# A four-layer gated decoder on one core: layer 2's expert features spread over the partitions, every eleventh into a chunk

## The chip, the core and the metric

The kernel runs as one program on one core of a Trainium2 chip. The metric is the device time of an execution in microseconds (us); the median of 13 runs of the kernel before is 1903.45 us, from 1896.32 to 1908.32. Beside these runs one execution was profiled, and every line of a profile below comes from it.

The names of the engines in the profile: PE is TensorE's matmul, PEld its weight load, DVE is VectorE, ACT is ScalarE, POOL is GpSimd, SP is SyncE, which issues most of the transfers. L1906 is line 1906 of the kernel.

## What is computed

64 sequences of 64 tokens with 128 features go through four layers. Each layer adds a gated attention branch to `x` and then a gated feed-forward branch, every branch on a layernorm of `x`. The change touches layer 2's feed-forward branch: a router picks two of eight experts for a token, every expert is a gated unit of 176 hidden features, and a ninth, shared expert is weighted by a sigmoid.

```python
def _L2_ffn_ref(hidden_states, gate_w, w_gate, w_up, w_down, sw_gate, sw_up, sw_down, shared_gate_w):
    E, K, I = (8, 2, 176)
    ...
    combine = jnp.sum(jax.nn.one_hot(topk_i, E, dtype=topk_w.dtype) * topk_w[..., None], axis=1)
    g = jnp.einsum('th,ehi->eti', x, w_gate)
    u = jnp.einsum('th,ehi->eti', x, w_up)
    eo = jnp.einsum('eti,eih->eth', jax.nn.silu(g) * u, w_down)
    out = jnp.einsum('te,eth->th', combine, eo)
    sg = jax.nn.sigmoid(jnp.einsum('th,oh->to', x, shared_gate_w))
    so = jax.nn.silu(x @ sw_gate) * (x @ sw_up) @ sw_down
    out = out + sg * so
```

The kernel computes all nine experts for every token. The nine times 176 features are one row of 1584 features, and each feature's hidden value is multiplied by its expert's weight for the token (zero for an expert that was not picked) ahead of the down projection.

## The kernel before, in words

**Groups, units and the planner.** The 4096 tokens are eight groups of 512 (4 tiles of 128). There are eight steps: 0, 2, 4 and 6 are the attention branches of layers 0 to 3, and 1, 3, 5 and 7 the feed-forward ones. A unit is one step of one group. The list `ORDER` (L2135) names the units in the order in which they are recorded: "50" is step 5, layer 2's feed-forward branch, of group 0. Nothing runs while units are recorded. Every operation goes into a plan (L299), which knows from the tiles what each operation depends on. `Plan.order` (L401) then writes one instruction stream for each engine: it walks through time with an estimated duration for each operation (`cost`, L221), and gives each engine the operation of the lowest rank that is ready, where the rank is essentially the place in the recording. So operations of several groups and layers stand mixed on each engine, and the engines run them in exactly the order that was written. Scratch tiles come from pools of fixed size (`SLOTS`, L41): 45 tiles of 2 KB a partition (in the profile `b2k`), 8 banks of PSUM (`ps`), and others; an operation that opens a tile waits in the plan until one is free. Where the plan sees TensorE idle, `keep_clock` (L482) fills the gap with matmuls of the identity into a free bank, which nobody reads; they carry line L2158.

**Layer 2's feed-forward unit** (L1896). `ln_T` normalizes and transposes the group into `xT`, 128 features by 512 tokens. `route` (L1847) computes the nine weights of each token, mostly on DVE. `spread` (L1885) transposes them (L1889), copies them out of PSUM (ACT, L1891) and writes them to a DRAM scratch `cwd` of 9 rows by 512 tokens (SP, L1893). Then come 13 chunks of features. In the kernel before, chunk c holds the features 128c to 128c+127 (the last one 48). A chunk's tile `cb` of 128 by 512 has in partition r the weight row of feature r's expert; it is loaded from `cwd` with one broadcast for each expert in the chunk (L1906), two or one a chunk, 20 a unit. A chunk is then two matmuls (L1914 and L1915, gate and up; one, L1911, for the last chunk), Silu on ACT (L1917), the product with the up part on DVE (L1918), the product with `cb` on POOL (L1919), and the down projection on TensorE (L1920), which accumulates over the chunks in one bank. The sum is copied out (L1922), transposed and added to `x`.

**The weights** (L1816) are loaded once. `wg` and `wu` lie as 128 input features by 1584 columns, and a chunk's stationary operand is 128 neighbouring columns of it. `wd` lies as 13 blocks of 128 features; L1833 loads it with 29 transfers.

Other lines that are spoken of below: L1236 and L1291 are layer 0's expert matmuls, and L1282 issues the loads of its one-hot rows (DRAM scratch `ohd`), which the products of L1289 read. L840 is the transpose of any step. L1663, L1674 and L1701 are the attention matmuls of layers 2 and 3. L1585 issues layer 1's feed-forward gathers from POOL, eight a unit.

Of the kernel before, what the change touches and what calls it, by code (L numbers as in the profile page):

```python
# [27 lines left out]
P = 128  # L28
# [5 lines left out]
GT = 512  # L34
# [730 lines left out]
def bc(ap, axis, n):  # L765

    ap = ap.unsqueeze(axis)
    shape = list(ap.shape)
    shape[axis] = n
    return ap.to_broadcast(shape)  # L770
# [8 lines left out]
def first_onehot(k, vals, best, rank, tag):  # L779

    nc = k.nc
    p, m, n = vals.shape
    eq = k.tile([p, m, n], tag=tag + "e")
    nc.vector.tensor_tensor(eq, vals, bc(best, 2, n), ALU.is_equal)
    nc.vector.tensor_tensor(eq, eq, bc(rank, 1, m), ALU.mult)
    top = k.tile([p, m], tag=tag + "t")
    nc.vector.tensor_reduce(top, eq, AX.X, ALU.max)
    oh = k.tile([p, m, n], tag=tag + "o")  # L790
    nc.vector.tensor_tensor(oh, eq, bc(top, 2, n), ALU.is_equal)
    return oh
# [42 lines left out]
def transpose4(k, src):  # L835

    ps = k.ps()
    k.plan.wait(src)
    for t in range(4):
        k.nc.tensor.transpose(ps[:, t * P : (t + 1) * P], src[:, t, :], k.ident)  # L840
    return ps


def ln_T(k, g):

    ps = transpose4(k, layernorm(k, g))
    xT = k.tile([P, GT], tag="xT")
    k.nc.scalar.copy(xT, ps)
    return xT
# [966 lines left out]
def l2_ffn_weights(k):  # L1816
    k.l2f = {"gate": k.load("l2f_gate")}

    last = k.l2f["last"] = k.fixed("w_l2f_last", [P, 112])
    k.nc.gpsimd.memset(last, 0.0)  # L1820
    at, end = k.done
    for n, name in enumerate(("wg", "wu")):
        t = k.l2f[name] = k.fixed("w_l2f_" + name, [P, 1536])
        k.nc.scalar.dma_start(out=t, in_=k.a["l2f_" + name][:, :1536])
        k.nc.scalar.dma_start(out=last[:, 64 * n : 64 * n + 48], in_=k.a["l2f_" + name][:, 1536:])
        k.plan.after = k.plan.ops[at + (end - at) * (n + 1) // 3]
    src = k.a["l2f_wd"]
    wd = k.l2f["wd"] = k.fixed("w_l2f_wd", [P, 13, P])
    for n in range(18):
        r = 88 * n  # L1830
        while r < 88 * n + 88:
            end = min(88 * n + 88, (r // P + 1) * P)
            k.nc.sync.dma_start(  # L1833
                out=wd[r % P : r % P + end - r, r // P, :], in_=src[r - 88 * n : end - 88 * n, n * P : (n + 1) * P]
            )
            r = end


def l2_ffn(k):
    nc = k.nc  # L1840
    E, I, HID = 8, 176, 9 * 176
    CH = [(c, min(P, HID - c)) for c in range(0, HID, P)]
    W = k.l2f

    gate = k.tg[:, 1, 2:3]

    def route(xT, g):  # L1847

        pr = k.ps()
        for t in range(TG):  # L1850
            nc.tensor.matmul(
                pr[:, t * (E + 1) : (t + 1) * (E + 1)], xT[:, t * P : (t + 1) * P], W["gate"], start=True, stop=True
            )
        lg = pr[:, : TG * (E + 1)].rearrange("p (t e) -> p t e", e=E + 1)
        pb = k.tile([P, TG, E], tag="pb")
        m = k.tile([P, 4, TG], tag="m")
        nc.vector.tensor_reduce(m[:, 0], lg[:, :, 0:E], AX.X, ALU.max)
        nc.vector.tensor_tensor(pb, lg[:, :, 0:E], bc(m[:, 0], 2, E), ALU.subtract)
        nc.scalar.activation(pb, pb, AF.Exp)
        nc.vector.tensor_reduce(m[:, 1], pb, AX.X, ALU.add)  # L1860
        nc.vector.reciprocal(m[:, 1], m[:, 1])
        nc.vector.tensor_tensor(pb, pb, bc(m[:, 1], 2, E), ALU.mult)
        nc.vector.tensor_reduce(m[:, 2], pb, AX.X, ALU.max)
        oh1 = first_onehot(k, pb, m[:, 2], k.rank8, tag="l2oh1")
        nc.vector.scalar_tensor_tensor(pb, oh1, -2.0, pb, ALU.mult, ALU.add)
        nc.vector.tensor_reduce(m[:, 3], pb, AX.X, ALU.max)
        oh2 = first_onehot(k, pb, m[:, 3], k.rank8, tag="l2oh2")

        nc.vector.tensor_tensor(m[:, 0], m[:, 2], m[:, 3], ALU.add)
        nc.vector.reciprocal(m[:, 0], m[:, 0])  # L1870
        nc.vector.scalar_tensor_tensor(m[:, 2], m[:, 2], gate, m[:, 0], ALU.mult, ALU.mult)
        nc.vector.scalar_tensor_tensor(m[:, 3], m[:, 3], gate, m[:, 0], ALU.mult, ALU.mult)
        cw = k.tile([P, TG, E + 1], tag="cw")
        nc.vector.tensor_tensor(oh1, oh1, bc(m[:, 2], 2, E), ALU.mult)
        nc.vector.tensor_tensor(oh2, oh2, bc(m[:, 3], 2, E), ALU.mult)
        nc.vector.tensor_tensor(cw[:, :, 0:E], oh1, oh2, ALU.add)

        sg = k.tile([P, TG], tag="sg1")
        nc.scalar.activation(sg, lg[:, :, E], AF.Exp, scale=-1.0)
        nc.vector.tensor_scalar(sg, sg, 1.0, None, ALU.add)  # L1880
        nc.vector.reciprocal(sg, sg)
        nc.vector.tensor_scalar(cw[:, :, E], sg, gate, None, ALU.mult)
        return cw

    def spread(cw):  # L1885

        pc = k.ps()
        for t in range(TG):
            nc.tensor.transpose(pc[: E + 1, t * P : (t + 1) * P], cw[:, t, :], k.ident)  # L1889
        cT = k.tile([E + 1, GT], tag="cwT")  # L1890
        nc.scalar.copy(cT, pc[: E + 1, :])  # L1891
        d = k.dram([E + 1, GT], "cwd")
        nc.sync.dma_start(out=d, in_=cT)  # L1893
        return d

    def unit(g):  # L1896
        xT = ln_T(k, g)
        cwd = spread(route(xT, g))
        py = k.ps()
        for c, (c0, cn) in enumerate(CH):  # L1900
            cb = k.tile([P, GT], tag="cb")
            r = c0
            while r < c0 + cn:
                e = r // I
                end = min(c0 + cn, (e + 1) * I)
                nc.sync.dma_start(out=cb[r - c0 : end - c0, :], in_=cwd[e : e + 1, :].to_broadcast([end - r, GT]))  # L1906
                r = end
            pg = k.ps()
            if cn < P:
                pu = pg[64 : 64 + cn]  # L1910
                nc.tensor.matmul(pg[: 64 + cn], W["last"], xT, start=True, stop=True)  # L1911
            else:
                pu = k.ps()
                nc.tensor.matmul(pg, W["wg"][:, c0 : c0 + cn], xT, start=True, stop=True)  # L1914
                nc.tensor.matmul(pu, W["wu"][:, c0 : c0 + cn], xT, start=True, stop=True)  # L1915
            h = k.tile([P, GT], tag="h")
            nc.scalar.activation(h[:cn], pg[:cn], AF.Silu)  # L1917
            nc.vector.tensor_tensor(h[:cn], h[:cn], pu, ALU.mult)  # L1918
            nc.gpsimd.tensor_tensor(h[:cn], h[:cn], cb[:cn], ALU.mult)  # L1919
            nc.tensor.matmul(py, W["wd"][:cn, c, :], h[:cn], start=(c == 0), stop=(c == len(CH) - 1))  # L1920
        yT = k.tile([P, TG, P], tag="yT")
        nc.scalar.copy(yT.rearrange("p t i -> p (t i)"), py)  # L1922
        xg = k.x[g].rearrange("p t d -> p (t d)")
        nc.vector.tensor_tensor(xg, xg, transpose4(k, yT), ALU.add)

    return unit
# [44 lines left out]
def l3_ffn(k):  # L1971
# [163 lines left out]
ORDER = [  # L2135
    (int(n), int(g))
    for n, g in (
        "02 00 03 01 06 04 10 05 11 20 07 21 30 31 40 12 41 50 13 51 16 22 14 60 15 61 23 70 26 32 17 24 "
        "71 42 25 33 36 27 43 34 46 52 35 44 62 45 37 53 56 47 63 54 66 55 64 65 72 57 67 73 76 74 75 77"
    ).split()  # L2140
]

# [1 line left out]
def program(tc, a):  # L2144
    with ExitStack() as es:
# [9 lines left out]
        for g in early:  # L2155
            nc.sync.dma_start(out=k.x[g], in_=xin[g])
        constants(k)
        plan.spare = (sys._getframe().f_lineno, k.ident, k.ident.t.writes[-1][0])  # L2158
        mixers = (l0_xattn, l0_ffn, l1_xattn, l1_ffn, l2_xattn, l2_ffn, l3_xattn)
        weights = (None, l0_ffn_weights, l1_xattn_weights, l1_ffn_weights, l2_xattn_weights, l2_ffn_weights,  # L2160
                   l3_xattn_weights)
        layers = [None] * 8
# [123 lines left out]
```

## Time and profile before

| | |
|---|---|
| median of 13 runs | 1903.45 us (1896.32 to 1908.32) |
| the profiled execution's own time | 1901.54 us |
| its span in the profile | 1899.8 us |
| mean granted TensorE clock | 0.975 of full speed |
| busy: PE, DVE, ACT, POOL | 1809.8, 1361.8, 1106.2, 1023.9 us |
| moved by DMA | 121.11 MB |

The span is what the profile's views add up to; the execution's own time is 1.7 us longer, and the median of the runs another 1.9 us. A line of the groups names the source line, the engine and operation, the tiles, the shapes and the count, then the busy time and the mean duration of one in ns, and last the idle time of the engine just ahead of it with what ended it. One float32 matmul in the program appears as two weight loads and two passes. [...]

### The profile page before, as it was taken

How to read it: one execution, taken by the hardware profiler on the slowest of the kernel's cores; microseconds unless marked ns; L12 is line 12 of the kernel's file. 1: busy time of each engine (PE TensorE's matmuls, PEld its weight loads, DVE VectorE, ACT ScalarE, POOL GpSimd, SP SyncE). 2: the span in 40 equal slices, each digit the busy share in tenths (PEclk: the TensorE clock that was granted, in tenths of full speed). 3: DMA queues.
4: the chain of work that ended last, by engine and by line, in shares of the span. 5: the costliest groups of instructions: out<-in, count | busy, mean ns of one | idle time of the engine just before them, and what ended most of it. 6: DMA issues, size and time to landing. Idle time of an engine off the chain costs nothing.

```text
span 1899.8 us, 44771 instructions
## 1 busy us (share of the span) xinstructions
PE 1809.8 (95%) x16701; PEld 1067.0 (56%) x16703; DVE 1361.8 (72%) x3194; ACT 1106.2 (58%) x2957; POOL 1023.9 (54%) x1655
## 2 busy tenths in 40 slices
PE   7999999999999999999999999999799999999996
PEld 4555456655555454655566655584466555555675
DVE  6786887678767477557786668769558876855567
ACT  6564446745374253733458743877467766867655
POOL 7772446644352443412638354856577478466546
PEclk8899999998999999999999999999899999999999
DMA  6302231013333321031210022000140034153121
GB/s 189 115 22 82 57 95 26 2 36 108 104 75 109 102 54 65 9 91 48 73 49 13 10 55 79 24 3 1 40 118 29 29 98 120 34 137 100 33 74 45
DMA packets 122231, 121.11 MB, mean 64 GB/s; under 512 B 58378, under 2 KB 78485, under 8 KB 122013
## 3 DMA queue, kind: packets, MB, share of 16 engines
q1 hardware_dynamic: 112541, 102.66, 19.2%
q10 hardware_dynamic: 6400, 9.25, 1.6%
q0 software_dynamic: 3072, 6.33, 1.2%
q8 instruction: 132, 2.16, 0.5%
q14 instruction: 86, 0.70, 0.1%
HBM read 98.22 MB, written 8.18 MB: 56 GB/s over the span
## 4 chain that ended last, share of the span: by engine, by line
PE 69%; DVE 9%; POOL 8%; ACT 4%; DMA 4%; issue 3%; another core or an unknown queue 1%; SPq 0%; ACTq 0%; DVEq 0%; POOLq 0%
PE ps L1236 11%; PE ps L1291 8%; PE ps L840 8%; POOL b L776 6%; PE ps L1920 5%; PE ps L1914 4%; PE ps L1915 4%; PE ps L1470 3%; PE ps L1701 3%; PE ps L1349 3%; PE ps L1457 2%; PE ps L1663 2%; PE ps L1386 2%; PE ps L1263 1%; DVE b2k L1289 1%
## 5 line engine op out<-in xcount | busy, mean ns | idle before, releaser
L776 POOL TENSOR_TENSOR b<-b,neghalf 128x8 f32<-128x8 f32 (+1 forms) x208 | 303.2, 1458 | 17.0
L1291 PE MATMUL ps<-b2k,w_l0f_oe 128*128 128x512 f32 x512 | 234.2, 601 | 3.6 <-DVE b2k L1289 2.4
L1236 PE MATMUL ps<-w_l0f_ve,b2k 128*128 128x512 f32 x512 | 236.3, 602 | 0.5 <-DVE b4k L1105 0.2
L775 POOL TENSOR_SCALAR b<-b 128x8 f32<-128x8 f32 (+1 forms) x208 | 44.3, 213 | 317.9 <-DVE b L804 193.2
L1289 DVE TENSOR_TENSOR b2k<-b2k,b2k 128x512 f32<-128x512 f32 x256 | 173.9, 729 | 28.1 <-PE ps L1291 13.3
L1242 DVE COPY_PREDICATED b2k<-b1k,ps 128x512 f32<-128x512 int32 x224 | 162.0, 727 | 43.4 <-PE ps L1236 25.7
L1919 POOL TENSOR_TENSOR b2k<-b2k,b2k 128x512 f32<-128x512 f32 (+1 forms) x104 | 130.8, 1281 | 106.7 <-DMA b2k<-cwd 59.0
L1104 DVE TENSOR_REDUCE b<-ps 128x8 f32<-128x512 f32 x224 | 146.9, 683 | 56.0 <-PE ps L1674 14.8
L1291 PEld LDWEIGHTS ps<-b2k,w_l0f_oe 128*128 128x128 f32 x512 | 93.7, 191 | 121.1 <-issue 80.6
L1107 ACT ACTIVATE b4k<-b4k 128x64 f32<-128x64 f32 x512 | 125.8, 250 | 47.1 <-DVE b4k L1105 44.4
L1105 DVE TENSOR_TENSOR b4k<-ps,b 128x512 f32<-128x512 f32 x224 | 149.5, 683 | 3.1 <-PE ps L840 2.2
L1236 PEld LDWEIGHTS ps<-w_l0f_ve,b2k 128*128 128x128 f32 x512 | 93.5, 191 | 101.8 <-issue 84.1
L840 PE MATMUL ps<-ident,b2k 128*128 128x128 f32 x896 | 133.6, 277 | 9.7 <-DVE b2k L1360 3.4
L840 PEld LDWEIGHTS ps<-ident,b2k 128*128 128x128 f32 x896 | 102.5, 141 | 68.9 <-issue 33.0
L840 PE MATMUL ps<-ident,b4k 128*128 128x128 f32 x896 | 127.8, 279 | 6.9 <-DVE b2k L1918 1.9
L840 PEld LDWEIGHTS ps<-ident,b4k 128*128 128x128 f32 x896 | 102.7, 142 | 51.2 <-issue 28.6
L1918 DVE TENSOR_TENSOR b2k<-b2k,ps 128x512 f32<-128x512 f32 (+1 forms) x104 | 70.2, 684 | 73.1 <-ACT b2k L1917 38.6
L1360 DVE TENSOR_TENSOR b2k<-ps,b 128x512 f32<-128x512 f32 x128 | 87.5, 687 | 30.7 <-POOL b L1357 17.0
L1354 DVE TENSOR_REDUCE b<-b2k 128x8 f32<-128x512 f32 x128 | 84.9, 678 | 27.8 <-ACT b2k L1351 25.0
L1920 PE MATMUL ps<-b2k,w_l2f_wd 128*128 128x512 f32 (+1 forms) x208 | 102.0, 608 | 2.9 <-POOL b2k L1919 2.8
L1689 ACT ACTIVATE b4k<-b4k 128x512 f32<-128x512 f32 x128 | 76.2, 630 | 48.2 <-DVE b4k L1105 47.8
L1440 POOL TENSOR_TENSOR b4k<-b4k,b 128x512 f32<-128x512 f32 x64 | 67.6, 1078 | 65.5 <-DVE b L1437 54.4
(368 smaller groups left out, 4090.0 us busy)
## 6 DMA issues: line engine op xcount, KB each, us to landing
b2k<-ohd SPq DMA_DIRECT2D x256, 128.0 KB
b2k<-cwd SPq DMA_DIRECT2D x40, 256.0 KB
b2k<-in_ctxT SPq DMA_DIRECT2D x32, 256.0 KB
b2k<-b2k SPq DMA_DIRECT2D x128, 64.0 KB
b2k<-b2k SPq DMA_DIRECT2D x32, 128.0 KB
b2k<-cwd SPq DMA_DIRECT2D x16, 224.0 KB
b2k<-cwd SPq DMA_DIRECT2D x16, 192.0 KB
b2k<-cwd SPq DMA_DIRECT2D x16, 160.0 KB
```

What stands on the lines that cost most here:

```text
L776: k.nc.gpsimd.tensor_tensor(out, out, k.neghalf[:, :n], ALU.pow)
L840: k.nc.tensor.transpose(ps[:, t * P : (t + 1) * P], src[:, t, :], k.ident)
L1104: nc.vector.tensor_reduce(mx, src, AX.X, ALU.max)
L1105: nc.vector.tensor_tensor(out, src, bc(mx, 2, S), ALU.subtract)
L1107: nc.scalar.activation(out[:, n, :], out[:, n, :], AF.Exp, accum_out=den[n])
L1236: nc.tensor.matmul(pe, xT[:, t * P : (t + 1) * P], W["ve"][:, e * 512 : (e + 1) * 512], start=True, stop=True)
L1242: nc.vector.copy_predicated(acc, bc(ohi[:, t * H : (t + 1) * H, e], 2, DH), pe.rearrange("p (h d) -> p h d", d=DH))
L1289: nc.vector.tensor_tensor(so, oT[c], pick[:, u, :], ALU.mult)
L1291: nc.tensor.matmul(py, W["oe"][:, n * P : (n + 1) * P], so, start=(n == 0), stop=(n == C * E - 1))
L1360: nc.vector.tensor_tensor(n.rearrange("p c (r d) -> p (c r) d", r=2), ps.rearrange("p (h d) -> p h d", d=DH), bc(r, 2, DH), ALU.mult)
L1919: nc.gpsimd.tensor_tensor(h[:cn], h[:cn], cb[:cn], ALU.mult)
L1920: nc.tensor.matmul(py, W["wd"][:cn, c, :], h[:cn], start=(c == 0), stop=(c == len(CH) - 1))
```

## The change

Chunk c, for c from 0 to 10, takes the features c, c+11, c+22 and so on up to 1407 of the eight routed experts: 128 features, and partition q holds feature 11q+c. Since 176 is 16 times 11, partition q belongs to expert q // 16 in all eleven chunks. So one tile `cbe`, with each of the eight weight rows on 16 partitions, serves eleven chunks, and a tile `cbs`, with the shared expert's row on all partitions, serves the last two. The stationary operands of L1914 and L1915 are views with a step of 11 columns. `wd` is loaded to match, in 19 transfers. Besides, `ORDER` lists the units in another sequence.

```diff
     for n, name in enumerate(("wg", "wu")):
-        t = k.l2f[name] = k.fixed("w_l2f_" + name, [P, 1536])
+        t = k.fixed("w_l2f_" + name, [P, 1536])
         k.nc.scalar.dma_start(out=t, in_=k.a["l2f_" + name][:, :1536])
+        k.l2f[name] = [t[:, c:1408:11] for c in range(11)] + [t[:, 1408:]]
...
-    for n in range(18):
-        r = 88 * n
-        while r < 88 * n + 88:
-            end = min(88 * n + 88, (r // P + 1) * P)
-            k.nc.sync.dma_start(
-                out=wd[r % P : r % P + end - r, r // P, :], in_=src[r - 88 * n : end - 88 * n, n * P : (n + 1) * P]
-            )
-            r = end
+    for n in range(16):
+        k.nc.sync.dma_start(
+            out=wd[8 * n : 8 * n + 8, 0:11, :], in_=src[:, n * P : (n + 1) * P].rearrange("(q c) d -> q c d", c=11)
+        )
+    for p0, c, n, r0, rows in ((0, 11, 16, 0, 88), (88, 11, 17, 0, 40), (0, 12, 17, 40, 48)):
+        k.nc.sync.dma_start(out=wd[p0 : p0 + rows, c, :], in_=src[r0 : r0 + rows, n * P : (n + 1) * P])
...
         cwd = spread(route(xT, g))
+        cbe = k.tile([P, GT], tag="cbe")
+        nc.sync.dma_start(out=cbe, in_=cwd[0:E, :].unsqueeze(1).to_broadcast([E, 16, GT]))
+        cbs = k.tile([P, GT], tag="cbs")
+        nc.sync.dma_start(out=cbs, in_=cwd[E : E + 1, :].to_broadcast([P, GT]))
         py = k.ps()
         for c, (c0, cn) in enumerate(CH):
-            cb = k.tile([P, GT], tag="cb")
-            r = c0
-            while r < c0 + cn:
-                e = r // I
-                end = min(c0 + cn, (e + 1) * I)
-                nc.sync.dma_start(out=cb[r - c0 : end - c0, :], in_=cwd[e : e + 1, :].to_broadcast([end - r, GT]))
-                r = end
+            cb = cbe if c < 11 else cbs
...
-                nc.tensor.matmul(pg, W["wg"][:, c0 : c0 + cn], xT, start=True, stop=True)
-                nc.tensor.matmul(pu, W["wu"][:, c0 : c0 + cn], xT, start=True, stop=True)
+                nc.tensor.matmul(pg, W["wg"][c], xT, start=True, stop=True)
+                nc.tensor.matmul(pu, W["wu"][c], xT, start=True, stop=True)
...
 ORDER = [
...
-        "02 00 03 01 06 04 10 05 11 20 07 21 30 31 40 12 41 50 13 51 16 22 14 60 15 61 23 70 26 32 17 24 "
-        "71 42 25 33 36 27 43 34 46 52 35 44 62 45 37 53 56 47 63 54 66 55 64 65 72 57 67 73 76 74 75 77"
+        "01 03 02 00 11 04 10 21 05 20 31 13 06 12 30 41 07 14 40 51 15 23 22 50 61 16 24 60 33 32 71 17 "
+        "25 43 42 70 34 26 44 35 53 52 27 45 36 54 46 37 55 63 62 47 56 64 57 65 66 73 72 67 74 75 76 77"
```

Since the plan takes the order of recording as its rank and the transfers as part of its timeline, the instruction streams of all engines come out in another sequence from the first microsecond on. What of each kind stands in them can be counted in the two programs without running them:

| instructions | before | changed |
|---|---|---|
| matmuls, without the identity ones of L2158 | 9350 | 9350 |
| identity matmuls of L2158: head, middle, end of the stream | 46, 15, 186 | 51, 1, 169 |
| switches from one tile size of the array to another | 584 | 581 |
| activation table loads on ACT | 98 | 82 |
| transfers issued by SP | 810 | 656 |
| matmuls of L1663, L1674 and L1701 in the first 15 twentieths of PE's matmuls, of 1600 | 496 | 688 |

## The prediction

> **What bounds the kernel.** I read the busy times of the engines first, then TensorE's groups, then a table of 50 us stretches, and last the waits on the tile that the change takes away. The first lines are from the page, the others from PE's and PEld's groups, each shape apart.
>
> ```profile
> span 1899.8 us, 44771 instructions
> PE 1809.8 (95%) x16701; PEld 1067.0 (56%) x16703; DVE 1361.8 (72%) x3194; ACT 1106.2 (58%) x2957; POOL 1023.9 (54%) x1655
> ```
> ```profile
> L1914 PE MATMUL ps<-b2k,w_l2f_wg 128*128 128x512 f32 x192 | 100.4, 605 | 2.5 <-issue 2.5
> ...
> L1920 PE MATMUL ps<-b2k,w_l2f_wd 128*128 128x512 f32 x192 | 93.0, 605 | 2.8 <-POOL b2k L1919 2.8
> ...
> L2158 PE MATMUL ps<-ident 128*128 128x128 f32 x494 | 67.2, 288 | 1.4 <-POOL ident L859 1.4
> ```
> ```profile
> L1701 PEld LDWEIGHTS ps<-b1k,b2k 128*64 128x64 f32 x2048 | 64.5, 138 | 24.5 <-issue 13.8 <-ACT b2k L1693 3.3 <-ACT b2k L1114 1.5
> ...
> L1914 PEld LDWEIGHTS ps<-b2k,w_l2f_wg 128*128 128x128 f32 x192 | 34.9, 192 | 39.5 <-issue 33.6 <-DVE b2k L1918 0.7 <-DVE b4k L1105 0.7
> ```
>
> TensorE is busy for 95% of the span, and the chain that ended last runs through PE for 69% of it. What can be won at all is its idle time, 1899.8 - 1809.8 = 90.0 us, plus the 67.2 us of identity matmuls that fill idle time, plus what the granted clock lost. The stretches show where that is (the columns: span, PE, PEld, DVE, ACT and POOL busy, clock, DMA share, GB/s):
>
> ```profile
> 650.00:700.00 50.00, 50.00 (x355) 24.93 (x353) 30.46 (x54) 23.74 (x96) 17.20 (x25) 1.00 0.12 30
> ...
> 1300.00:1350.00 50.00, 39.43 (x434) 21.61 (x432) 37.62 (x80) 27.30 (x78) 41.84 (x51) 0.90 0.09 24
> 1350.00:1400.00 50.00, 45.39 (x471) 30.56 (x471) 32.31 (x106) 33.28 (x82) 23.36 (x34) 0.96 0.12 36
> ...
> 1550.00:1600.00 50.00, 46.77 (x389) 26.44 (x390) 37.62 (x109) 29.15 (x53) 40.26 (x68) 1.00 0.56 142
> ...
> 1850.00:1900.00 50.00, 34.73 (x280) 28.45 (x278) 40.02 (x55) 26.81 (x37) 33.15 (x27) 0.91 0.14 43
> ```
>
> Summed over all 38 stretches, PE idles 14.6 us before 100 us, 25.5 us from 100 to 1300, 29.2 us from 1300 to 1750, and 20.9 us after; of the identity matmuls 13.9 us lie in the head and 49.3 us after 1750. The clock lost (one minus the granted clock, times 50 us) 28 us between 100 and 1750. The head waits for first loads and the end for layer 3's global maxima; neither is touched. So the change acts on the middle, which has 54.7 + 3.9 + 28 = 87 us of slack in 1650, one third of its idle time in the last 450 us, where the attention of layers 2 and 3 and all but two of the layer 2 FFN units stand.
>
> **What the change takes away, by the waits.** POOL's multiplications wait 59 us for the tile, but PE waits only 2.8 us for POOL (L1920's row above). The lines: the waits; SP's queue for one whole unit; the chain in two other units.
>
> ```profile
> POOL b2k L1919 <- DMA b2k<-cwd: 59.0, 14, 20.0
> ```
> ```profile
> 540.89 12.79 SPq L1906 DMA_DIRECT2D b2k<-cwd  x20
> ```
> ```profile
> 1584.19 8.32 DMA b2k<-cwd
> ```
> ```profile
> 1654.48 4.16 DMA b2k<-cwd
> ```
>
> Of the 59 us, 20.0, 17.5 and 9.4 are waits ahead of a unit's first or second multiplication: the time until the weights have been routed, written out and loaded. One load takes 4.16 us there, and the changed unit still needs one (128 x 512, the size of the old full chunk). Only the rest, 12 us of POOL, belongs to later chunks. The sum, step by step:
>
> 1. *Loads of L1906, 160 to 16.* PE's 2.8 us behind L1920 are the direct term; 0.7 of them is behind a first load and stays, and the 8.32 us piece of the chain, where the loads of a unit queue for each other, shrinks towards 4.16. I take **-3 us**; bounds 0 (POOL has idle time to catch up: 54% busy) and -7 (2.8 + 4.16).
> 2. *SP's queue.* 20 issues take 12.79 us, 0.64 each: 144 fewer free 92 us of SP (with `wd`, 29 to 19, 154 issues fewer). What stands behind them is L1282's loads for layer 0: from 610 to 625 us the two alternate on SP, DMA is 84 to 99% busy in 615 to 625, and PE then loses 0.50 + 0.59 us behind L1289. **-2 us**; bounds 0 and -5 (all DVE waits of L1289 for `ohd` are 6.5 us, and not all stand there).
> 3. *Traffic.* 13 chunks of up to 256 KB a group (24.8 MB) become 4.0 MB, of 121.11. DMA's share is 20%, so outside the stretches of step 2 nothing waits: **0**; bound -3.
> 4. *`wd`.* Now mostly 8 partitions x 11 blocks a transfer. In the old kernel it was issued from 491 to 505 us and first used at 546: 40 us of cover, **0**; should the new first unit follow closer, at most the 13 us of issuing.
> 5. *Tables.* 16 fewer table loads at 1283 ns are 20.5 us of ACT. The chain has ACT for 4% of 1900 = 76 us of its 1106 busy, 7%: **-1.4 us**; bounds 0 and -20.5.
> 6. *Identity matmuls.* 247 to 221: 26 x 272 ns (67.2/247) = 7.1 us. They are put where the plan sees PE idle, so fewer say that it sees less waiting; whether the chip does is another matter. **-4 us**; bounds 0 and -7.
> 7. *Stationary operands with a step of 11.* 11 chunks x 2 matmuls x 2 passes x 8 groups = 352 weight loads read one element in each 44 bytes. No PE row has such a step. Passes of 512 columns follow each other at 430 ns (8 passes of L1920 make 3.44 us of the chain) and a load of 128 columns takes 190, beside the pass before. So 240 ns of cover: **0**. A load's duration grows from 138 ns at 64 columns to 192 at 128, 0.84 ns a column on 84 fixed; were every column four times as slow, 84 + 430 = 514, and the cover is gone: +84 x 352 = +30 us. That is the other bound; below nothing there is no reason for a gain.
> 8. *The order.* In the stream of the changed program 688 instead of 496 of the 1600 attention matmuls of layers 2 and 3 stand in the first three quarters: 192 of 1104, 17%, leave the crowded end. The idle time of 1300 to 1750 (29.2 us) and its lost clock (11.5 us) times 17% is **-7 us**. No row prices a whole new order: bounds -25 (the idle rate of 100 to 1300, 2.1%, there as well: 29.2 - 9.5 = 20, plus half the clock) and +35 (rival 3).
>
> [...]
>
> Sum: -3 - 2 - 1.4 - 4 - 7 = -17.4. From the profiled execution's 1901.5 that is 1884; with the 1.9 us to the median of the runs, **1886 us**. More than half of it is steps 6 and 8, the new sequence: the transfers that the change is named after are mostly hidden.
>
> **Rivals.**
> *Rival 1, hidden anyway:* POOL, SP and DMA had room, and the new sequence wins in one place what it loses in another. For it: PE waits for POOL's products only 2.8 us. Against: the uneven idle time. 1903.45 - 3 = about 1901 us.
> *Rival 2, slower, the strided weights:* a load of L1914/L1915 that takes longer than the 430 ns between passes sets the pace. It decides the sign from (17.4/352 = 49 ns above) 480 ns on; at 514 ns it adds 30 us to the forecast: about 1915 us. For it: no row with such a step. Against: more than twice the present duration is covered.
> *Rival 3, the sequence is worse:* layer 1's gathers. The chain has pieces at 1336.86 (9.70 us), 1347.42 (4.98) and 1490.41 (6.72) in which ACT and PE stand while L1585 issues its gathers on POOL, 21.4 us in two of the eight units. If the new sequence puts the other units also beside work that waits so, five at 7 us are +35; two or three more are likely enough: 1903 + 18 = about 1921 us without the gains of step 8.
>
> **How the numbers follow.** Forecast 0.55 (its own range 1866 to 1899), rival 1 0.15, rival 2 0.08, rival 3 0.22. About 0.2% is what a measurement of this kernel can tell from no change: 3.8 us. Faster: the forecast 0.55 and a third of rival 1, 0.60; same 0.11 (the rest of it and a little of rival 3); slower 0.29. The range reaches from the forecast's low end, with steps 5 and 8 at half of their gains more, to rival 3: **1864 to 1922**, with about 0.07 left out below and 0.12 above.
>
> **What would show it.** Right: no wait of POOL for `cwd` but the units' first; PE's idle time between 1300 and 1750 below 25 us; weight loads of L1911 and L1912 (the old L1914 and L1915) under 430 ns and their passes 430 apart; the end after 1750 as before; DMA near 100 MB. Wrong: passes of these lines further apart (rival 2), longer pieces beside L1585, or PE idle over 60 us between 100 and 1750 (rival 3); or PE busy no lower and idle no lower (rival 1). The forecast fails above all if PE's idle time doesn't follow the share of attention work in the end.

## The result and the profile after

The changed kernel takes **1925.08 us** (median of 14 runs, 1915.90 to 1931.61); in the same sets of runs the kernel before takes 1900.64 us (62 runs). The ratio is 1.0126, 95% interval 1.0111 to 1.0141: slower by 24.4 us. The forecast was 1886 us and faster, and its range ended at 1922.

The profiled execution of the changed kernel took 1935.2 us, 10 us above the median and the longest of all; its span is 1933.5 us, 33.7 more than before. First the page and TensorE's groups (busy time, mean ns of one | idle time just ahead):

```profile
span 1933.5 us, 44189 instructions
...
PE 1829.5 (95%) x16649; PEld 1116.8 (58%) x16651; DVE 1356.5 (70%) x3194; ACT 1090.7 (56%) x2941; POOL 1036.6 (54%) x1655
```
```profile
L1911 PE MATMUL ps<-b2k,w_l2f_wg 128*128 128x512 f32 x192 | 103.4, 620 | 0.1
...
L1917 PE MATMUL ps<-b2k,w_l2f_wd 128*128 128x512 f32 x192 | 95.7, 613 | 0.1
L2155 PE MATMUL ps<-ident 128*128 128x128 f32 x442 | 63.4, 298 | 1.9 <-POOL ident L859 1.4 <-DVE b1k L1091 0.5
```
```profile
L1701 PEld LDWEIGHTS ps<-b1k,b2k 128*64 128x64 f32 x2048 | 69.2, 143 | 30.2 <-issue 17.6 <-ACT b2k L1693 6.0 <-ACT b2k L1914 1.7
...
L1911 PEld LDWEIGHTS ps<-b2k,w_l2f_wg 128*128 128x128 f32 x192 | 58.3, 315 | 20.0 <-issue 4.6 <-DVE b4k L1105 1.0 <-DVE b L1856 0.5
```

L1911 is the old L1914, L1917 the old L1920, L2155 the old L2158. The 176 strided weight loads of L1911 take 326 ns in the mean (the row's 315 holds 16 packed ones of 190) in place of 192. TensorE's matmuls no longer wait for POOL ahead of the down projection (0.1 us idle, before 2.8); its weight loads there, all 40.2 us of which run beside other passes, still wait 6.4 us for POOL, before 8.8. Next the waits of POOL and what the chain holds for the tile, the old L1919 now being L1916:

```profile
POOL b2k L1916 <- DMA b2k<-cwd: 21.3, 4, 8.6
```
```profile
1395.32 4.51 DMA b2k<-cwd
1727.66 4.25 DMA b2k<-cwd
```

59.0 us in 14 waits have become 21.3 in 4, and a piece of the chain is one load long. So what the change is named after did happen. The stretches (span, PE, PEld, DVE, ACT and POOL busy, clock, DMA share, GB/s) show where the time went:

```profile
650.00:700.00 50.00, 49.97 (x284) 28.89 (x283) 28.41 (x60) 27.39 (x43) 29.50 (x33) 1.00 0.08 23
1050.00:1100.00 50.00, 45.43 (x530) 30.45 (x527) 43.09 (x108) 37.43 (x103) 19.29 (x26) 0.99 0.10 32
1100.00:1150.00 50.00, 40.85 (x374) 25.50 (x374) 31.09 (x79) 17.34 (x87) 24.89 (x57) 0.84 0.16 46
1250.00:1300.00 50.00, 44.01 (x642) 30.53 (x636) 40.51 (x95) 32.20 (x76) 24.57 (x35) 0.90 0.06 18
1300.00:1350.00 50.00, 49.55 (x673) 34.09 (x673) 38.20 (x93) 41.25 (x116) 39.60 (x61) 0.96 0.04 12
...
1600.00:1650.00 50.00, 42.42 (x414) 30.29 (x413) 35.15 (x99) 34.31 (x65) 15.74 (x34) 0.89 0.07 20
```

1300 to 1350, the worst stretch of the old kernel but the end, is full now; 1050 to 1150, 1250 to 1300 and 1600 to 1650 are the holes, with a low clock in or behind each. In each of them stand gathers of L1585: they begin at 1086.1, 1096.3, 1288.1 and 1618.4 us. The worst hole, in the chain:

```profile
1093.98 1.05 ACT b4k L1689 x2
1095.04 3.31 another core or an unknown queue
1098.35 0.02 issue
1098.37 0.59 ACT b2k L1693
1098.96 0.53 ACT b4k L1689
1099.49 9.53 another core or an unknown queue
```

While POOL issues two units' sixteen gathers, ACT stands for 3.31 and 9.53 us with no releaser that the view names; PE waits 3.80 and 7.47 us for ACT, and DVE 13.6 us for PE. "Another core or an unknown queue" only says that no instruction ended when the wait did. The trace's semaphore updates say more: ACT waits there for the semaphore that PE's matmuls count up. The matmul that ends at 1093.51 us has its update at 1098.35, and those that end at 1095.22, 1095.74, 1100.66 and 1103.48 have theirs at 1109.02 to 1109.20, 6 to 14 us late. In two later runs of the same streams (e11 and e14 below) the same four updates come 0.01 to 0.02 us after the ends. A matmul's end is modelled in the profile, so whether the matmuls or only their updates are late isn't shown.

### The profile page after: what moved, and what is told of

The parts are those of the page before. It is cut to its first block, busy times and chain, and to the rows that moved or that the text cites. A ratio compares the mean times of both kernels' runs of the same rounds, so it can differ in the third digit from the quotient of the medians.

```text
span 1933.5 us, 44189 instructions
## 1 busy us (share of the span) xinstructions
PE 1829.5 (95%) x16649; PEld 1116.8 (58%) x16651; DVE 1356.5 (70%) x3194; ACT 1090.7 (56%) x2941; POOL 1036.6 (54%) x1655
## 2 busy tenths in 40 slices
DMA packets 109025, 99.30 MB, mean 51 GB/s; under 512 B 55800, under 2 KB 75907, under 8 KB 108811
## 4 chain that ended last, share of the span: by engine, by line
PE 71%; DVE 11%; POOL 6%; ACT 5%; issue 3%; DMA 3%; another core or an unknown queue 1%; SPq 1%; DVEq 0%; ACTq 0%; POOLq 0%
PE ps L1236 10%; PE ps L1291 9%; PE ps L840 8%; PE ps L1917 5%; PE ps L1912 4%; PE ps L1911 4%; PE ps L1349 3%; POOL b L776 3%; PE ps L1701 3%; PE ps L1470 3%; PE ps L1386 2%; PE ps L1457 2%; PE ps L1263 2%; PE ps L1663 2%; PE ps L2155 1%
## 5 line engine op out<-in xcount | busy, mean ns | idle before, releaser
L1236 PE MATMUL ps<-w_l0f_ve,b2k 128*128 128x512 f32 x512 | 244.0, 615 | 4.5 <-ACT b2k L1183 2.4
L1291 PE MATMUL ps<-b2k,w_l0f_oe 128*128 128x512 f32 x512 | 228.2, 596 | 3.1 <-DVE b2k L1289 2.8
L1289 DVE TENSOR_TENSOR b2k<-b2k,b2k 128x512 f32<-128x512 f32 x256 | 168.7, 712 | 16.6 <-DMA b2k<-ohd 7.9
L1916 POOL TENSOR_TENSOR b2k<-b2k,b2k 128x512 f32<-128x512 f32 (+1 forms) x104 | 129.0, 1273 | 43.8 <-DMA b2k<-cwd 21.3
L840 PE MATMUL ps<-ident,b4k 128*128 128x128 f32 x896 | 134.4, 284 | 13.5 <-ACT b4k L1689 7.0
L840 PEld LDWEIGHTS ps<-ident,b2k 128*128 128x128 f32 x896 | 104.1, 143 | 62.9 <-issue 37.5
L840 PEld LDWEIGHTS ps<-ident,b4k 128*128 128x128 f32 x896 | 104.9, 145 | 61.1 <-issue 33.3
L840 PE MATMUL ps<-ident,b2k 128*128 128x128 f32 x896 | 132.5, 280 | 7.2 <-DVE b2k L1360 2.6
L1915 DVE TENSOR_TENSOR b2k<-b2k,ps 128x512 f32<-128x512 f32 (+1 forms) x104 | 70.2, 684 | 68.7 <-PE ps L1912 37.7
L1917 PE MATMUL ps<-b2k,w_l2f_wd 128*128 128x512 f32 (+1 forms) x208 | 104.7, 615 | 0.1
L1912 PE MATMUL ps<-b2k,w_l2f_wu 128*128 128x512 f32 x192 | 103.4, 621 | 0.4 <-ACT b2k L1914 0.4
```

The source lines that it names most:

```text
L1236: nc.tensor.matmul(pe, xT[:, t * P : (t + 1) * P], W["ve"][:, e * 512 : (e + 1) * 512], start=True, stop=True)
L1289: nc.vector.tensor_tensor(so, oT[c], pick[:, u, :], ALU.mult)
L1291: nc.tensor.matmul(py, W["oe"][:, n * P : (n + 1) * P], so, start=(n == 0), stop=(n == C * E - 1))
L1912: nc.tensor.matmul(pu, W["wu"][c], xT, start=True, stop=True)
```

## The experiments

Every ratio is to the kernel before on the same chip, with a 95% interval. The chips turned out to be of two kinds: on some the kernel before takes 1898 to 1901 us (the result above, e1 to e4, e13 to e15), on others 1859 to 1861 us (e5 to e12, e16, e17). Each of the experiments' five chips was used at one time only, so the chip and the time can't be told apart. The texts on record name theories by letters; each letter is said where it comes up.

**First set: the strided weights (theory A) or the sequence (theory B).** e1 is the changed kernel with the columns of `wg` and `wu` packed in the host's layout, so that a chunk's operand is contiguous again; the streams are the same. e2 is the reverse, the kernel before with a step of 11 in its operands.

```diff
# e1, in the changed kernel (the columns are reordered in _layout)
-        k.l2f[name] = [t[:, c:1408:11] for c in range(11)] + [t[:, 1408:]]
+        k.l2f[name] = [t[:, c * P : (c + 1) * P] for c in range(12)]
# e2, in the kernel before
-                nc.tensor.matmul(pg, W["wg"][:, c0 : c0 + cn], xT, start=True, stop=True)
+                cols = slice(c, 1408, 11) if c < 11 else slice(c0, c0 + cn)
+                nc.tensor.matmul(pg, W["wg"][:, cols], xT, start=True, stop=True)
```

> The changed kernel, its instruction streams unchanged, with the columns of wg and wu laid out ahead of time so that each chunk's 128 columns are neighbours. Theory A (the weight loads with a step of 11, which take 323 ns in the changed kernel's trace where 190 stood before, are exposed wherever the work before them is short): the loads go back to 190 ns and most of the loss goes, 1900 to 1908 us. Theory B (the new sequence of units costs the time, the loads are hidden under 430 ns passes): within 4 us of the changed kernel's 1925.

Measured: 1921.84 us, ratio **1.0099** (1.0069 to 1.0130).

> The kernel before, its instruction streams unchanged, with the gate and up matmuls of the first eleven chunks reading their stationary operand at a step of 11 columns; features and expert weights no longer belong together, so the numbers of that branch are others. Theory A: 10 to 25 us above the kernel before. Theory B: within 4 us of the kernel before.

Measured: 1903.75 us, ratio **1.0013** (0.9994 to 1.0031). The step of 11 costs 0.13% (e2) to 0.27% (1.0126 less e1's 1.0099), 2.5 to 5 us, and neither can be told from nothing. Theory A falls. e2's weight loads, shown next, are as long as the changed kernel's, and its matmuls of the same line wait no more:

```profile
L1915 PEld LDWEIGHTS ps<-b2k,w_l2f_wg 128*128 128x128 f32 x192 | 58.0, 315 | 20.2 <-issue 3.9 <-ACT b2k L1918 1.4 <-DVE b L804 0.4
```
```profile
L1915 PE MATMUL ps<-b2k,w_l2f_wg 128*128 128x512 f32 x192 | 103.7, 622 | 0.7 <-ACT b2k L1918 0.7
```

e3 and e4 exchange the two `ORDER` lists and nothing else: e3 is the changed kernel with the old list, e4 the kernel before with the new one.

> The changed kernel with the list of units of the kernel before. Theory A: 10 to 20 us above the kernel before, for the strided loads stay. Theory B: at the kernel before or up to 8 us below it, the direct gain of the prediction (its steps 1 to 3: 5 us).

Measured: 1928.74 us, ratio **1.0130** (1.0101 to 1.0159). It is 27.5 us above the kernel before, outside both theories' ranges. And it is a loss of another kind than the changed kernel's: the plan writes 368 identity matmuls (736 passes) in place of 247, 99.7 us against 67.2, while PE idles 78.6 us of the span, before 90.0.

```profile
L2155 PE MATMUL ps<-ident 128*128 128x128 f32 x736 | 99.7, 287 | 3.0 <-POOL ident L859 1.4 <-ACT b2k L1914 1.1 <-DVE w_l0f_oe L2094 0.4
```

> The kernel before, with its 20 loads a unit and packed weights, recorded in the changed kernel's sequence of units. Theory A: within 6 us of the kernel before. Theory B: 15 to 30 us above it, as the changed kernel.

Measured: 1961.06 us, ratio **1.0316** (1.0285 to 1.0348), 59.8 us above the kernel before and again outside both ranges. The new sequence alone is not what makes the changed kernel good or bad: with the old mapping it is the worst of all, and the old sequence with the new mapping is no better than the new. So theory B, as it was put, misses here too: the time goes with the streams that the plan writes from list and mapping together. Why e4 is the worst stays open.

**Second set: loads or sequence.** e5 keeps the old instruction streams (but for the place of a few small operations on DVE): of the 20 loads of a unit it leaves 3, and the products read one of two fixed tiles (packed weights; fewer `b64` and `b256` slots to make room). Theory C: the loads are a gain that the sequence gives back; theory D: having fewer loads itself costs.

```diff
+                if r == 0:
+                    k.plan.alt[k.plan.ops[-1].n] = ((), {"out": cbe, "in_": rows})
+                elif c < 11:
+                    k.plan.alt[k.plan.ops[-1].n] = None
...
+            if c < 11:
+                k.plan.alt[k.plan.ops[-1].n] = ((h[:cn], h[:cn], cbe, ALU.mult), {})
```

(`alt` gives an operation other operands, or leaves it out, when the finished streams are issued.)

> The kernel before with its own instruction streams on TensorE, ACT and POOL (DVE differs in the place of a few small operations), the features laid out ahead of time so that each chunk holds every eleventh one in neighbouring columns; of the 18 loads of the first eleven chunks of a unit one is left, of the eight experts' rows into one of two fixed tiles. So 3 loads a unit in place of 20 and no new sequence. Theory C (fewer loads are a gain of steps 1 to 3 of the prediction, about 5 us, and the plan's new sequence gives back more): 3 to 8 us below the kernel before, PE without waits behind L1920. Theory D (the loads themselves, one later and larger first load or a held tile, cost the time): 5 us or more above it.

Measured: 1873.31 us, ratio **1.0072** (1.0050 to 1.0094). Slower by 13.6 us, with 17 loads a unit fewer and the same order: theory C's gain isn't there, and theory D's loss is. A cause can be seen in its trace, and the third set tests it. e6 and e7 only exchange two neighbours in the `ORDER` of the kernel before (`16 22` and `46 52`). Theory C' takes the sequence for a lottery, in which any change costs 1 to 3%; D' takes it for smooth.

> The kernel before, computing the same in the same way, with two neighbours in the list of units exchanged (22 ahead of 16). Theory C' (the sequence that the plan writes is a lottery of 1 to 3%, whatever is changed in it, and the list of the kernel before is a lucky draw): anywhere from 1895 to 1950 us, more likely above 1905. Theory D': within 6 us of the kernel before.

Measured: 1858.17 us, ratio **0.9987** (0.9967 to 1.0007), as D' says.

> The kernel before with another two neighbours exchanged (52 ahead of 46). The plan writes 319 identity matmuls instead of 247. Theory C': 1910 to 1950 us. Theory D': within 6 us of the kernel before.

Measured: 1889.40 us, ratio **1.0169** (1.0137 to 1.0201). Two units exchanged cost more than the whole change: C' in size. But 18.6 of the 29.7 us are identity matmuls (85.8 us, before 67.2), so a good part of this price stood in the plan. One exchange of each kind is too few to say how often one costs. e8 is the changed kernel, packed, with a list found by searching for an early end in the kernel's own plan (the first line of the list is kept).

> The changed kernel with packed weights (as e1) and a list of units that the plan itself ends 1% earlier with than with the changed kernel's list (some 500 lists tried in the plan, starting from the changed kernel's), 201 identity matmuls. Theory C and C': 1885 to 1905 us, at or below the kernel before. Theory D: it stays above 1912 us, near e1.

Measured: 1855.94 us, ratio **0.9988** (0.9969 to 1.0007). There is no gain. That the other sequence takes the loss away isn't shown by this: on this kind of chip the changed kernel as it is loses only 0.25% (e11 below), and e8 has packed weights besides.

**Third set: DVE and POOL, the kind of chip, the control.** In e5's trace DVE's operation L1977 (`low`, the mask of layer 3's attention) took 11.33 us in one unit, elsewhere 0.2 to 0.4. e9 repeats e5, and e10 computes `low` on ACT at the same places. Theory E: POOL, no longer stopped by loads, shuts DVE out; theory F: the cost is spread.

```diff
         nc.vector.tensor_scalar(low, mask, 0.0, -1e20, ALU.is_equal, ALU.mult)
+        k.plan.alt[k.plan.ops[-1].n] = ((low, mask, AF.Copy), {"scale": 1e20, "bias": -1e20}, "scalar", "activation")
```

> The same kernel as the earlier one with the old streams and 3 loads a unit, on the same chip as the next one, for the pair. Both theories: ratio to before near the 1.0072 of its first run; DVE's 128x256 tensor_scalar of L1977 again over 10 us once, while POOL runs L1932 nine times back to back, and PE idle 9 to 10 us ahead of L1667.

Measured: 1875.08 us, ratio **1.0084** (1.0054 to 1.0113).

> The kernel with the old streams and 3 loads a unit, but the operation that DVE was kept from for 11.33 us (low, L1977) is computed on ACT, eight times some 0.4 us, at the same places. Theory E (DVE and POOL shut each other out): the products of POOL, no longer held up by loads, run without a gap, and DVE's operation waits for the end of the whole run; without it the 9.6 us of PE ahead of L1667 go, with the clock they cost, and the ratio falls by 0.5 to 0.7% to between 0.999 and 1.003. Theory F (fewer loads cost in many small places, or the other long operations of DVE take its place): stays at 1.005 or more.

Measured: 1862.50 us, ratio **1.0021** (1.0002 to 1.0040). Theory E holds: three quarters of e9's loss go with one operation. The timelines of e9 on DVE, POOL and PE (start, us, engine, line, operation, count, idle ahead):

```profile
1563.20 0.25 DVE L1714 RECIPROCAL b<-ps 128x16 f32<-128x16 f32 x1
1563.36 11.34 DVE L1977 TENSOR_SCALAR b1k<-b1k 128x256 bf16<-128x256 int32 x1
1574.63 0.21 DVE L1716 TENSOR_TENSOR b2k<-ps,b 128x64 f32<-128x64 f32 x1
```
```profile
1562.28 11.06 POOL L1932 TENSOR_TENSOR b2k<-b2k,l2f_cbe 128x512 f32<-128x512 f32 x9
1573.30 1.26 POOL L1932 TENSOR_TENSOR b2k<-b2k,b2k 128x512 f32<-128x512 f32 x1
```
```profile
1575.23 2.21 PE L1667 MATMUL ps<-b2k,b2k 32*64 32x256 f32 x32 [9.57 <-DVE b2k L1716]
```

and of e10, POOL and then the stretch 1550 to 1600:

```profile
1558.30 11.11 POOL L1932 TENSOR_TENSOR b2k<-b2k,l2f_cbe 128x512 f32<-128x512 f32 x9
```
```profile
1550.00:1600.00 50.00, 49.22 (x503) 29.92 (x503) 36.12 (x90) 39.02 (x74) 42.45 (x83) 1.00 0.17 50
```

In e9 L1977 ends at 1563.36 + 11.34 = 1574.70, 0.14 us after POOL's run of ten multiplications, and PE waits 9.57 us; in e9 the stretch has PE 40.40 and the clock at 0.90. In e10 PE is busy 49.22 us of that stretch beside the same run of POOL. In e9, then, DVE was held to the end of ten instructions, not of one; by what mechanism, the rows don't show.

e11 is the changed kernel again, unaltered, on the quicker kind of chip. Theory G: the sequence loses by itself; theory K: it loses beside the gathers of L1585.

> The changed kernel itself, unaltered, on the chip of this call. The earlier chips differed in one thing: where before took 1901 us, PE idled 18 to 27 us beside the 64 gathers of L1585, and where it took 1860 us, 1 to 3 us, whatever the kernel. Theory G (the sequence loses by itself, in many places): ratio 1.010 to 1.015 on either kind of chip. Theory K (the sequence loses because it puts two units' gathers one behind the other, 1086 to 1106 us, where PE idled 9.9 us and the clock fell to 0.84): if PE's idle time beside L1585 is under 5 us on this chip, the ratio is 1.007 or less; on the slower kind of chip 1.010 or more, and nothing is told apart.

Measured: 1865.19 us, ratio **1.0025** (1.0006 to 1.0044). The chain of this trace has no piece without a releaser. The stretches of this trace around the same two units' gathers, which begin at 1070.2 and 1080.4 us here:

```profile
1034.00:1084.00 50.00, 50.00 (x628) 34.78 (x620) 46.36 (x120) 41.21 (x115) 19.36 (x26) 1.00 0.11 32
1084.00:1118.00 34.00, 32.02 (x334) 19.41 (x333) 27.66 (x67) 14.54 (x86) 25.94 (x59) 1.00 0.25 67
```

PE idles 2 of 84 us there, at full clock, where the other trace had 13.7 of 100 and a clock of 0.84. Theory K holds here. No update of PE's semaphore is over 0.3 us late in this trace; in the first trace of the changed kernel 54 of some 2470 are over 0.5 us late, and all of them lie within 4 us of a unit's gathers. e12 is the control for e8: the kernel before with a searched list. The plan, which the kernel makes while it is built, ends at 1774.7 us for the kernel before and 1778.1 for the changed one; searched, it ends at 1765.9 and 1759.6. Theory M: the mapping is worth nothing beyond its sequence; N: it is worth something.

> The kernel before, with only its sequence of units searched in the plan as the changed kernel's was in the run at 0.9988: the plan's own end falls from 1774.7 to 1765.9 us (there from 1778.1 to 1759.6). It is the control for what the mapping itself is worth. Theory M (nothing beyond the sequence): 0.994 to 0.999, at least as good as the changed kernel searched. Theory N (the spread features are worth something that the published sequence hid): 1.000 or more here, so that what the search gained there was the mapping's.

Measured: 1852.42 us, ratio **0.9962** (0.9948 to 0.9977): theory M. The plan had put the searched changed kernel 6 us ahead of this one; on the chip it is not.

**Fourth set, on the slower kind of chip: the gathers taken out.** In e14 and e15 each gather is a plain load of the same size, from fixed rows, issued by SP. Both the kind of the transfer and its issuer change, so the two can't be told apart.

```diff
+                if meth == "indirect_dma_start":
+                    args, kw, eng, meth = (), {"out": kw["out"], "in_": kw["in_"][0:P, :]}, "sync", "dma_start"
```

> The kernel before, unaltered, for a profile on the chip of this call. Theory K (what the changed kernel loses beyond 0.25% is time beside the gathers of L1585): if the chip is of the faster kind (some 1860 us), the difference to its profile at 1899.8 us lies in steps at the eight groups of gathers and nowhere else, and adds up to about 42 us, where the changed kernel's adds up to 69. Theory G (the changed sequence loses everywhere): the difference is spread over the span.

Measured: 1901.29 us; a chip of the slower kind, so the comparison with the quicker kind could not be made with it. It serves for the one below.

> The changed kernel, all streams as they are, but each of the 64 gathers of L1585 is a plain load of 128 fixed rows, issued by SP at the same place of the program instead of by POOL. It leaves out the pick of the expert's rows, nothing else. Theory K: on a chip where before takes about 1901 us it falls to 1856 to 1868 (ratio to before 0.977 to 0.983), and to 1.000 to 1.005 of the next kernel; on a chip where before takes about 1860 it changes by less than 5 us (ratio 0.999 to 1.003). Theory G: on the slower kind of chip it stays 1.009 or more above the next kernel.

Measured: 1867.50 us, ratio **0.9849** (0.9818 to 0.9880).

> The kernel before with the same replacement. Theory K: on the slower kind of chip 1853 to 1862 us (ratio 0.974 to 0.980); on the faster kind within 5 us of before. Theory G: the gathers' cost is the same in both kernels, so the changed one stays 1.009 or more above this one on the slower kind.

Measured: 1853.85 us, ratio **0.9774** (0.9742 to 0.9806). The gathers cost the kernel before 1898.1 - 1853.9 = 44 us. The changed kernel was not run with its gathers on this chip; at its ratio of 1.0126 it would take 1922.0 us, so that they cost it some 1922.0 - 1867.5 = 55. Both kernels then stand within 8 us of what they take with gathers on the quicker kind of chip (1859 to 1861 and 1865), so the gathers account for the difference between the chips; taking them out on the quicker kind was not tried. But e14 is not within 0.5% of e15, as theory K had it: 0.9849/0.9774 = 1.0077 (1.003 to 1.012, the two intervals combined), between K's 0.5% and the 0.9% of theory G, with both in the interval. So theory K explains a part, and e14 and e15 alone don't tell how large a one.

Since the streams are the same with and without gathers, the start of one and the same ACT instruction can be compared in both traces. The difference grows beside the gathers (up to some 30 us behind a unit's last) and elsewhere by under 2 us at a place, with one exception: in the changed kernel's pair it grows by 7.5 us in the first 100 us, where no gather stands, so the profiled execution owes that part of its length to something else.

| kernel (trace with gathers - without) | start of a unit's gathers, us: growth of the difference, us | sum |
|---|---|---|
| before (e13 - e15) | 411: 4.0; 461: 2.8; 1086: 11.0; 1334 and 1345: 15.6; 1388: 3.8; 1489: 2.5; 1528: 4.5 | 44.2 |
| changed (its first trace - e14) | 387: 5.0; 541: 1.9; 1086 and 1096: 18.2; 1288: 8.5; 1382: 5.7; 1535: 6.5; 1618: 13.2 | 59.0 |

**Fifth set.** The two searched kernels, together on one chip.

> The changed kernel with the searched sequence (packed weights) a second time, beside the kernel before with a searched sequence: both so far only on the faster kind of chip, and in different calls. On the slower kind (before some 1900 us): theory K says that a sequence has a price beside the gathers of L1585 that the plan's search did not see, so the ratio may move by up to 1% either way from 0.9988, by as much as the time beside the gathers differs from before's 47 us. On the faster kind: 0.997 to 1.001 again. Theory G: the same ratio on either kind.

Measured: 1859.51 us, ratio **0.9994** (0.9970 to 1.0019).

> The kernel before with the searched sequence, same call. Its gathers stand in the same places as before's, so theory K says that the ratio stays at 0.994 to 0.999 on either kind of chip. Against the run before this one: at or below it (the features' spread worth nothing beyond the sequence), or above it by over 0.3% (worth something).

Measured: 1853.89 us, ratio **0.9961** (0.9944 to 0.9979). It was the quicker kind again. The kernel before with a searched sequence is 0.4% quicker than the kernel before, and the changed one searched is 0.3% slower than it (1859.51/1853.89): on this kind of chip the mapping is worth nothing beyond its sequence. On the slower kind the searched ones weren't tried.

## Why the prediction was wrong

The step that failed is **step 8, the order**, with the sign of the sum behind it. It took the idle time of 1300 to 1750 for a matter of how much attention work stands there, and 17% of it as the gain, with the rest of the middle unchanged. The windows 100 to 1300 and 1300 to 1750 of four traces, the kernel before, the changed one, e15 and e14 (columns as above):

```profile
100.00:1300.00 1200.00, 1174.54 (x10831) 667.55 (x10830) 874.15 (x1830) 645.58 (x2062) 561.06 (x819) 0.99 0.19 55
1300.00:1750.00 450.00, 420.81 (x3865) 251.54 (x3863) 321.43 (x891) 306.88 (x600) 296.43 (x522) 0.97 0.26 71
```
```profile
100.00:1300.00 1200.00, 1152.76 (x10536) 660.90 (x10534) 876.27 (x1877) 631.66 (x1990) 577.55 (x839) 0.98 0.18 53
1300.00:1750.00 450.00, 429.37 (x3957) 283.12 (x3958) 296.89 (x797) 301.91 (x642) 282.80 (x465) 0.95 0.09 27
```
```profile
100.00:1300.00 1200.00, 1179.54 (x10997) 669.68 (x10998) 895.01 (x1866) 660.37 (x2095) 556.43 (x820) 1.00 0.20 55
1300.00:1750.00 450.00, 439.31 (x4182) 267.49 (x4182) 331.79 (x930) 329.39 (x628) 269.49 (x508) 0.99 0.29 78
```
```profile
100.00:1300.00 1200.00, 1170.47 (x10972) 678.53 (x10974) 905.00 (x1939) 658.46 (x2083) 565.88 (x837) 1.00 0.19 54
1300.00:1750.00 450.00, 436.68 (x3930) 288.64 (x3926) 300.57 (x828) 298.73 (x604) 270.56 (x484) 0.99 0.11 34
```

From them PE's idle time in us, with the kernel before once more on the chip of e14 and e15 (e13), and the lost clock as the prediction counts it, from stretches of 50 us:

| | idle, 100 to 1300 | idle, 1300 to 1750 | lost clock, both |
|---|---|---|---|
| before | 25.5 | 29.2 | 28 |
| before (e13) | 27.6 | 23.9 | 26 |
| before without gathers (e15) | 20.5 | 10.7 | 6 |
| changed | 47.2 | 20.6 | 42 |
| changed without gathers (e14) | 29.5 | 13.3 | 10 |

In 1300 to 1750 idle time did fall, by 8.6 us, as step 8 said. But the reason was another: without gathers the old kernel idles only 10.7 us there. Its five units of gathers in that stretch made most of the hole, not the crowd of attention. The new sequence has three there and five before 1300, and the price went with them: 100 to 1300 idles 21.7 us more, and of its 47.2 us 17.7 go when the gathers are taken out (47.2 - 29.5; in the old kernel 5.0 to 7.1). The lost clock follows the holes, 14 us more than before. (The traces without gathers are 47 to 69 us shorter than those with, so their windows hold somewhat later work.) Without gathers the changed sequence still idles 11.6 us more than the old.

So in place of step 8's -7 us the new streams cost some 19 to 22, the 24.4 us less the 2.5 to 5 of the strided weights. How much of the 24.4 lies beside the gathers is not settled closely: 9 us by the ratios with and without them (1.0126 - 1.0077; 0 to 18 by the intervals), 15 by the starts of ACT's instructions (59.0 - 44.2; but e1's trace of the same streams gives some 51 in place of the 59.0), 19 by the quicker kind of chip (1.0126 - 1.0025; 15 to 24). The rest, 5 to 17 us, is in the sequence and the weights, and what in the sequence costs it stays open. The traces show that PE's updates come late beside a gather on one kind of chip; why, and why not on the other, they don't show.

The other steps:

- *1, loads:* the wait went as forecast (2.8 to 0.1 us ahead of the matmuls of the down projection), the time did not follow. In e10, where all but `low` is kept, the change of loads costs 0.02 to 0.40%, and in e9 a wait that POOL lost came back as one of DVE's behind POOL (11.34 us). -3 didn't come; rival 1, hidden anyway, describes this step. In the changed kernel's own trace no `low` is over 1.18 us, so that collision isn't part of its 24.4 us.
- *2, SP's queue:* DVE's wait of L1289 for `ohd` is 7.9 us, before 6.5. No gain.
- *3, traffic:* 99.30 MB, before 121.11; right, and no gain showed. (The step's 24.8 and 4.0 MB count 1024 x 1024 bytes; in the profile's unit they are 26.0 and 4.2.) *4, `wd`:* no wait for it in the trace; right.
- *5, tables, and 6, identity matmuls:* ACT is busy 15.5 us less and the identity matmuls 3.8 us less, where 20.5 and 7.1 were counted. The span grew all the same, and no run takes these two steps apart. Fewer identity matmuls weren't a sign of fewer waits.
- *7, strided operands:* right in the main: 0 came out as 2.5 to 5 us, not clear of nothing. A strided load takes 326 ns in the mean and 351 at most, under the 429 to 430 ns from the start of one pass to that of the next (so for 315 of the 384 passes of L1911 and L1912; 313 of them last 592 ns, so passes overlap). Its bound of +30 us didn't come. The 0.84 ns a column behind that bound is shaky: loads of the same 128 columns take 141 ns on L840.

Of the list of what would show it, POOL's waits (all four ahead of a unit's first product), the loads under 430 ns, DMA and idle time below 25 us between 1300 and 1750 (20.6) came. But PE idles 47.2 + 20.6 = 67.8 us between 100 and 1750, over the 60 that the list gave as the sign of rival 3. The sign of rival 1 came as well (PE busy 1829.5 us, before 1809.8; idle 104.0, before 90.0), so that sign didn't tell the two apart. And the prediction's "one third of its idle time" in the last 450 us is 29.2 of 54.7 us, over half: the hole that it had to explain was larger than it said. Rival 3 named the gathers of L1585 and priced two or three more bad units at 18 us, 1921 us. It was right in mechanism for a good part of the loss and nearly in size, with a chance of 0.22; that the size came so near is partly luck, as 5 to 17 us lie elsewhere. Its evidence, three pieces of the chain worth 21.4 us, was in the profile of before: I read them as what might be added and not as what the 29.2 us already were. They stand in three units, not two, and taking the gathers out showed that all eight had been costing 44 us.

## What to carry to other kernels

Before idle time is put down to what stands in a crowded stretch, list its gaps by what runs beside them: here 16.3 of the 29.2 us fell between a unit's first gather of L1585 and 3 us behind its last, and that would have warned that moving units moves the price along. Where a view names no releaser, look up the semaphore that is waited for. Where a planner writes the whole order, a change to the work is two changes; measure it with the streams kept, and give the old kernel the same search of its order, before anything is credited to it. And a wait that is taken from an engine off the critical path lets that engine run without gaps, which can shut out its neighbour, as POOL's ten multiplications did with DVE's `low` for 11.34 us in e9.

## What the runs showed of the hardware that was not expected

- Eight gathers issued by POOL cost 2 to 13 us a unit on one kind of chip (16 to 18 for two units one behind the other), 44 us in the old kernel and some 51 to 59 in the changed one; on other chips the same streams lose almost nothing there (from a unit's first gather to 3 us behind its last PE idles 26.7 us in all in the changed kernel's first trace, 1.1 in e11's).
- Beside these gathers the updates of PE's semaphore come up to 14 us after the modelled ends of its matmuls in the changed kernel's first trace; in e11 and e14 none is over 0.3 us late.
- A DVE `tensor_scalar` of 128 x 256 that takes 0.2 to 0.4 us elsewhere was held for 11.34 us (e9; 11.33 in e5) by ten POOL multiplications that ran back to back.
- A weight load of 128 columns with a step of 44 bytes takes 326 ns in place of 192; 58.3 - 34.9 = 23.4 us more on L1911 and about as much on L1912, and the time grew by 2.5 to 5 us in all, which can't be told from nothing.
